# A planned order for all engines in a convolution and attention kernel

## The chip, the cores and the metric

The kernel runs on one core of a Trainium2 chip. The time is the device time of one execution in microseconds (us), as the median of several runs. The core has five engines that work side by side, each through its own list of instructions: TensorE (PE: matrix products; PEld: the loading of its weights), VectorE (DVE), ScalarE (ACT), GpSimd (POOL) and SyncE (SP), which here only issues DMA transfers.

## The reference

All numbers are 32-bit floats. The input x has 16 samples of 256 channels on a 32 by 32 picture, so 1024 tokens. Four layers follow each other; cut to what matters:

```python
def attention(x, ...):               # layers 0 and 2
    h = group_norm(x)                # 8 groups
    q, k, v = wq @ h, wk @ h, wv @ h
    a = softmax(q.T @ k / sqrt(256))
    return x + proj(a @ v)

def gate(x):                         # layer 1
    m, M = mean(x, channels), max(x, channels)
    r = relu(conv3x3([m, M], w1, b1))
    return x * sigmoid(conv3x3(m + M + r, w2, b2))

def clipped(x):                      # layer 3, q and k of 32 channels
    e = clip(q.T @ k / sqrt(32), -10, 10)
    return gamma * (v @ softmax(e).T) + x
```

## The kernel before, in words

The weights are folded first (`fold`): query and key weights of a layer become one matrix m, value and projection weights one matrix wvp, so that an attention needs the products x m (tiles t_l, in banks tb, ta, tc, tf), x wvp (vb, va, vc, vf), the logits (sb, sa, sc, sf) and the weighted sum (b, af, c). Each of these is a product of 2 by 2 blocks, done with seven block products instead of eight (`seven`, `weighted`); sums of blocks are made on VectorE ahead of it (`combine` at L924 to L927 for x, `logits` for t, `weighted` for the exponentials, `value_sums`). Nearly all products are recorded by one helper at L577. Their results lie in eight PSUM banks, and ScalarE (copies, L696 for logits, L765 to L781 for the weighted sum) and VectorE (additions, L627 and L749) bring them to SBUF.

Samples go through two streams, even and odd (`stream(0)`, `stream(1)`), the second 30 steps behind the first; `in_turn` records one step of each by turns. The program has constants (W_PLANES to W_AV3) that set how many steps a stage is held back. So the order in which the program records the products is tuned by hand. A repeat, in which each stream does one sample, takes about 329 us, and there are eight of them, less the ends.

Group normalisation (`group_norm`) is a chain of small instructions: bn_stats over x on VectorE (L114), aggregates (L117), transposes, rstd on GpSimd (L138), a_l and bb_l (L141 to L144) and the normalisation, half of x on VectorE (L147), half on ScalarE (L150). Between layers a sample goes to DRAM and back with another layout: `send` stores mid_x in four pieces and loads x (L536, L540). Each sample's x is loaded a second time in another layout, tokens xr (`load_tokens`, L470), to which the attention's results are added. The mean for the gate is made on ScalarE, row by row, into a scrap tile named junk (L1043).

At the start two weight matrices raw_l0 and raw_l2, w3 (printed as w), x of samples 0 and 1, small vectors vec, sc, vcol and qb, and an index tidx are loaded. `fold3` scales w3 (L414), copies parts of it into w3qk on GpSimd (L425) and makes biases; `build_toep` makes matrices for the 3 by 3 convolutions on GpSimd from tidx and sc (L85 to L103); `right_sums` makes sums of weight blocks on GpSimd or VectorE (L290 to L298). `in_strips` spreads a bias (strips, L395 and L403).

What sets the order: the framework's scheduler takes the recorded program and gives each engine a fixed list, in which it may move instructions past each other by its own estimates. Three pins limit it. `keep_in_program_order` holds single instructions (toeplitz rows, copies of weights, w3qk, the first statistics of sample 1) at their recorded place; `behind_folds` puts the normalisation of sample 0 on ScalarE behind the folded weights' copies; `in_traced_order` chains all instructions of the last sample's layer 3 on TensorE, VectorE and ScalarE in recorded order, which `ending()` writes out by hand: score products s (L1135), the copies t_qk (L1122 to L1128), its weighted sums b_end, af_end, c_end with acc_end (L1234), and the additions of biases to the stored tokens (L493).

Of the kernel before, what the change touches and what calls it, by code (L numbers as in the profile page):

```python
# [13 lines left out]
ALU = mybir.AluOpType  # L14
AX = mybir.AxisListType

P = 128
C = 256
CC = C // P
# [4 lines left out]
TPH = HALF // P  # L24
GROUP = 32
DQK = 32
G4 = P // DQK
PH = P // 2
# [11 lines left out]
L2_GAMMA, L2_BETA, L2_BQ, L2_BK, L2_BP = range(5, 10)  # L40
NVEC = 10
OFFSET = 30


W_PLANES, W_GATE1, W_GATE2, W_SEND1, W_NORM1, W_NORM2, W_NORM3, W_SEND2, W_EXP, W_AV, W_AV3 = 9, 1, 2, 4, 2, 10, 4, 7, 2, 2, 0
# [6 lines left out]
SIZES = 16384.0  # L52
REACH = 1.0
CHECKS = 3 + 2 * CC


class Const:
# [26 lines left out]
    def build_toep(self, tc, work, tidx):  # L84

        nc = tc.nc
        for k in range(3):
            for tap in range(9):
                w = self.sc[:, S_W1 + 9 * k + tap : S_W1 + 9 * k + tap + 1]
                if tap == 0:  # L90
                    one = self.toep[:, k, :]
                else:
                    one = work.tile([P, STRIP], FP, tag="tap", name=f"tap_{k}_{tap}")
                tc.keep_in_program_order(
                    nc.gpsimd.tensor_scalar(one, tidx, float(tap), w, ALU.is_equal, ALU.mult)
                )
                if tap:
                    nc.gpsimd.tensor_tensor(self.toep[:, k, :], self.toep[:, k, :], one, ALU.add)
            yield
        for g in range(1, NG):  # L100
            nc.gpsimd.tensor_copy(self.toep[:, 2 + g], self.toep[:, 2])
        nc.vector.tensor_scalar(self.neg_b2, self.sc[:, S_B2 : S_B2 + 1], -1.0, None, ALU.mult)
        yield  # L103


def group_norm(nc, k, small, xt, out, gamma, beta, nm, keep=None, parts=1, behind=None):

    st = small.tile([P, CC, 2, 6], FP, tag="st", name=f"st_{nm}", bufs=2)  # L110
    mv = k.moments
    for c in range(CC):
        for h in range(NH):
            first = nc.vector.bn_stats(st[:, c, h, :], xt[:, c, h * TPH : (h + 1) * TPH])  # L114
            if keep is not None:
                keep(first)
        nc.vector.bn_aggr(mv[:, 2 * c : 2 * c + 2], st[:, c, :, :])  # L117
    row = small.tile([P, GROUP], FP, tag="row", name=f"row_{nm}", bufs=2)
    nc.vector.transpose(row, mv)
# [20 lines left out]
    a = small.tile([P, CC], FP, tag="a", name=f"a_{nm}")  # L140
# [4 lines left out]
    for i in range(parts):  # L145
        ts = slice(i * NT // parts, (i + 1) * NT // parts)
        nc.vector.tensor_scalar(  # L147
            out[:, 0, ts], xt[:, 0, ts], a[:, 0:1], bb[:, 0:1], ALU.mult, ALU.add
        )
        other = nc.scalar.activation(  # L150
            out[:, 1, ts], xt[:, 1, ts], AF.Identity, bias=bb[:, 1:2], scale=a[:, 1:2]
        )
        if behind is not None:
            behind(other)
    yield


# [50 lines left out]
def fast_path(nc, tc, k, bad, x, w_l0, w_l2, w_l3, qk_bias, v_bias, tap_idx, out):  # L208
# [5 lines left out]

    B = x.shape[0]
    with ExitStack() as ctx:
        wts = ctx.enter_context(tc.tile_pool(name="wts", bufs=1))
        chan = ctx.enter_context(tc.tile_pool(name="chan", bufs=3))
        tokp = ctx.enter_context(tc.tile_pool(name="tokp", bufs=3))
        qkvp = ctx.enter_context(tc.tile_pool(name="qkvp", bufs=2))  # L220
        expp = ctx.enter_context(tc.tile_pool(name="expp", bufs=3))
        combp = ctx.enter_context(tc.tile_pool(name="combp", bufs=2))
        tcp = ctx.enter_context(tc.tile_pool(name="tcp", bufs=2))
        work = ctx.enter_context(tc.tile_pool(name="work", bufs=4))
        small = ctx.enter_context(tc.tile_pool(name="small", bufs=4))
        dram = ctx.enter_context(
            tc.tile_pool(name="dram", bufs=2, space=bass.MemoryType.DRAM)
        )
        ps_m = ctx.enter_context(
            tc.tile_pool(name="ps_m", bufs=8, space=bass.MemoryType.PSUM)  # L230
        )

        def bank(nm):
            return ps_m.tile([P, HALF], FP, tag="m", name=nm)
# [34 lines left out]
        w3 = wts.tile([P, CC, 2 * DQK + C], FP, name="w3")  # L269
# [3 lines left out]
        tidx = wts.tile([P, STRIP], FP, name="tidx")  # L273
# [26 lines left out]
        def whole(w, nm):  # L300

            full = work.tile([P, CC, C], FP, tag="oc", name=f"full_{nm}", bufs=3)
            tc.keep_in_program_order(nc.vector.tensor_copy(full, w))
            nc.vector.tensor_tensor(full[:, 0, P:], w[:, 1, P:], w[:, 0, P:], ALU.subtract)
            return full

        copied = []

        def fold(nm, which, base):


            w = raw[nm]
            wt = expp.tile([P, 3, CC, C], FP, tag="e", name=f"wt_{nm}")

            def transposed(j):
                for o in range(CC):
                    ps = bank(f"wtp_{nm}_{j}_{o}")
                    for c in range(CC):
                        nc.tensor.transpose(
                            ps[:, c * P : (c + 1) * P],  # L320
                            w[:, c, j * C + o * P : j * C + (o + 1) * P],
                            k.ident,
                        )
                    copy = nc.scalar.copy if nm == "l0" else nc.vector.tensor_copy
                    copied.append(copy(wt[:, j, o, :], ps[:, :C]))

            def multiplied(dst, left, right, scale):
                for c in range(CC):
# [82 lines left out]

        def fold3():

            tc.keep_in_program_order(  # L414
                nc.vector.tensor_scalar(
                    w3[:, :, :DQK], w3[:, :, :DQK], DQK**-0.5, None, ALU.mult
                )
            )
            for g in (0, G4 - 1):
                s = slice(g * DQK, (g + 1) * DQK)  # L420
                nc.vector.tensor_scalar(qb[s], qb[s], DQK**-0.5, None, ALU.mult)
            for i in range(2):
                for j in range(2):
                    tc.keep_in_program_order(
                        nc.gpsimd.tensor_copy(  # L425
                            w3qk[:, :, i, (i ^ j) * DQK : (1 + (i ^ j)) * DQK],
                            w3[:, :, j * DQK : (j + 1) * DQK],
                        )
                    )
            ps = bank("bias3")  # L430
            for c in range(CC):
# [7 lines left out]
            for o in range(CC):  # L439
                for c in range(CC):  # L440
# [4 lines left out]
                        start=(c == 0),  # L445
                        stop=(c == CC - 1),
                    )
            tc.keep_in_program_order(
                nc.vector.tensor_tensor(qb, ps[:, CC : CC + 1], qb, ALU.add)
            )  # L450
            nc.vector.tensor_tensor(bcol3, ps[:, :CC], vcol[:, 2, :], ALU.add)
            nc.vector.scalar_tensor_tensor(bcol3, bcol3, gam, bcol2, ALU.mult, ALU.add)
            in_strips(bcol3, bstrip3, "l3")
# [116 lines left out]
        def product(terms, fresh=True, lone=True):  # L570
# [4 lines left out]
            for i, (out, pairs) in enumerate(terms):  # L575
                for m, (left, right) in enumerate(pairs):
# [10 lines left out]
                    elif m == 0 and not lone:  # L587
# [5 lines left out]
                            ),  # L593
                            reason="the first product clears the bank's flags",
                        )

        def in_traced_order(start):

            engines = mybir.EngineType.PE, mybir.EngineType.DVE, mybir.EngineType.Activation
            before = {}  # L600
            for ins in nc.cur_bb.bb.instructions[start:]:
                if ins.engine not in engines:
                    continue
                if ins.engine in before:
                    tc.add_manual_dep(
                        ins,
                        before[ins.engine],
                        mybir.DependencyInfo(
                            mybir.DependencyClass.NoSync, mybir.DependencyReason.DATA
                        ),  # L610
                        reason="the last sample's order",
                    )
                before[ins.engine] = ins.name

        def seven(go, copy, block, banks, left, right):

# [196 lines left out]
        def alike(w, nm):  # L813


            sq = work.tile([P, HALF], FP, tag="oc", name=f"sq_{nm}", bufs=3)
            tc.keep_in_program_order(
                nc.vector.tensor_tensor(sq.rearrange("p (c o) -> p c o", c=CC), w, w, ALU.mult)
            )
            yield from pause()  # L820
            ps = bank(f"size_{nm}")
            for c in range(CC):
# [169 lines left out]
                then(h, tt.rearrange("p h c n -> p h (c n)"))  # L992
            count(ri, nm)

        def behind_folds(ins):

            tc.add_manual_dep(
                ins.ins,
                copied[-1].ins.name,
                mybir.DependencyInfo(  # L1000
                    mybir.DependencyClass.NoSync, mybir.DependencyReason.DATA
                ),
                reason="the weights' copies come first",
            )

        def head(b):

            fetch(b)
            xt = loaded.pop(b)
            by_chunk = xt.rearrange("p t c n -> p c t n")  # L1010
            xr = tokens[b] = load_tokens(b)
            keep = tc.keep_in_program_order if b == 1 else None
            yield from group_norm(
                nc,
                k,
                small,
                by_chunk,
                by_chunk,
                L0_GAMMA,
                L0_GAMMA + 1,  # L1020
                f"l0_{b}",
                keep,
                1 if b else NH,
                None if b else behind_folds,
            )
            ready[b] = xt, xr

# [68 lines left out]
        def clipped_attend(xt, y, lane, b):  # L1096
# [316 lines left out]
            if b == B - 1:  # L1413
                while running:
                    yield
                start = len(nc.cur_bb.bb.instructions)
                ending()
                in_traced_order(start)
                return

            steps = values(lane, left, right_of(*folded["l3"]), f"l3_{b}")
# [91 lines left out]
        for _ in in_turn([in_turn(streams), rest]):  # L1513
# [7 lines left out]
        nc.vector.tensor_scalar(  # L1521
            bad, some[0:1, :], -1.0, float(P * (3 * B * NT + CHECKS)), ALU.mult, ALU.add
        )


def general_path(nc, tc, k, x, w_l0, w_l2, w_l3, qk_bias, v_bias, out):
# [308 lines left out]
```

## Time and profile before

| | before |
|---|---|
| median of 3 runs | 2680.28 us (2677.83 to 2680.78) |
| the profiled execution's own time | 2683.05 us |
| its span | 2681.3 us |
| TensorE busy, weight loads busy | 99%, 88% |
| VectorE, ScalarE, GpSimd busy | 80%, 50%, 3% |
| granted TensorE clock | 0.997 of full speed |

A page of the profile gives the busy time of each engine, the chain of work that ended last, and groups of instructions by line and tile. A timeline lists instructions with start and duration, and in brackets how long the engine stood idle before and what released it. Tile names are cut at their numbers: x_0 and x_12 are both x, and t_l is the same tile for both attention layers. A matrix product in 32-bit floats has two records. Times of TensorE's ends are modelled, so distances between starts are the safer reading.

### The profile page before, as it was taken

Reading aid. Unit: us, or ns where it says so; the run is one execution under the profiler, and the core shown is the slowest. Engines: PE = TensorE matmul, PEld = TensorE weight load, DVE = VectorE, ACT = ScalarE, POOL = GpSimd, SP = SyncE. Lnnn points to the kernel's source line nnn. Section 1 sums busy time; section 2 is a strip of 40 time slices with the busy share of each in tenths; the row PEclk is TensorE's granted clock in tenths of the full one; section 3 lists DMA queues with packets and bytes.
Section 4 is the critical chain, followed back from the end, with each engine's and each line's share of the span. In section 5 each row is a group of like instructions: output and inputs, shape, how many; then the busy total and the mean of one; then the engine's idle time right before and its main releaser. Section 6 shows DMA issues by size and latency. Waiting matters only on the chain.

```text
span 2681.3 us, 47925 instructions
## 1 busy us (share of the span) xinstructions
PE 2646.6 (99%) x18998; PEld 2361.7 (88%) x18998; DVE 2149.9 (80%) x4180; ACT 1332.2 (50%) x2825; POOL 68.5 (3%) x172
## 2 busy tenths in 40 slices
PE   8999999999999999999999999999999999999998
PEld 7888898888988889989889898988989889898897
DVE  7888887888778887788867889678887788868776
ACT  4454455544465445554455544554454544545443
POOL 4100000000000000000000000000000000000000
PEclk9999999999999999999999999999999999999999
DMA  4021211212021120211201212112111121101111
GB/s 116 1 64 48 59 29 36 60 40 76 12 55 49 40 72 9 56 48 48 64 17 48 64 34 63 32 32 64 48 48 32 32 64 48 48 17 32 48 40 41
DMA packets 135878, 123.08 MB, mean 46 GB/s; under 512 B 12768, under 2 KB 126688, under 8 KB 135648
## 3 DMA queue, kind: packets, MB, share of 16 engines
q1 hardware_dynamic: 133776, 118.76, 16.1%
q8 instruction: 153, 2.51, 0.4%
q10 hardware_dynamic: 1872, 1.18, 0.1%
q14 instruction: 77, 0.63, 0.1%
HBM read 69.58 MB, written 50.33 MB: 45 GB/s over the span
## 4 chain that ended last, share of the span: by engine, by line
PE 89%; DVE 7%; ACT 1%; issue 1%; DMA 1%; POOL 0%; SPq 0%; DVEq 0%; ACTq 0%
PE b_l L577 16%; PE sb_l L577 12%; PE af_l L577 11%; PE c_l L577 11%; PE sc_l L577 8%; PE vb_l L577 5%; PE sf_l L577 4%; PE sa_l L577 4%; PE vc_l L577 3%; PE tb_l L577 3%; PE s L1135 2%; PE tc_l L577 2%; PE vf_l L577 2%; PE va_l L577 2%; PE qk L1109 1%
## 5 line engine op out<-in xcount | busy, mean ns | idle before, releaser
L577 PE MATMUL sb_l<-t_l,x 128*128 128x256 f32 x1024 | 255.9, 381 | 0.0
L577 PE MATMUL b_l<-vt,e_l 128*128 128x128 f32 x2048 | 250.1, 275 | 0.0
L577 PEld LDWEIGHTS b_l<-vt,e_l 128*128 128x128 f32 x2048 | 242.6, 192 | 4.9 <-DVE acc_l L749 2.3
L696 ACT COPY e_l<-sb_l 128x512 f32<-128x512 f32 x256 | 150.1, 586 | 141.9 <-PE sb_l L577 141.1
L706 ACT ACTIVATE e_l<-e_l 128x512 f32<-128x512 f32 x256 | 159.8, 631 | 121.7 <-DVE e_l L627 119.8
L577 PEld LDWEIGHTS sb_l<-t_l,x 128*128 128x128 f32 x1024 | 185.4, 191 | 32.2 <-issue 10.3
L708 ACT ACTIVATE e_l<-e_l 128x1024 f32<-128x1024 f32 x128 | 135.2, 1056 | 114.3 <-DVE e_l L627 113.6
L627 DVE TENSOR_TENSOR e_l<-sc_l,e_l 128x512 f32<-128x512 f32 x128 | 88.0, 687 | 125.4 <-PE sc_l L577 98.7
L577 PE MATMUL c_l<-tv,cb_l 128*128 128x129 f32 x1504 | 185.8, 276 | 0.0
L577 PEld LDWEIGHTS c_l<-tv,cb_l 128*128 128x128 f32 x1504 | 176.5, 191 | 6.8 <-issue 5.7
L627 DVE TENSOR_TENSOR e_l<-sb_l,e_l 128x512 f32<-128x512 f32 x256 | 165.7, 680 | 4.8 <-ACT e_l L696 0.5
L493 ACT ACTIVATE xr<-xr,bstrip 128x128 f32<-128x128 f32 (+1 forms) x376 | 138.1, 435 | 50.6 <-DVE xr L500 50.6
L773 ACT COPY acc_l<-af_l 128x256 f32<-128x256 f32 x94 | 34.8, 371 | 231.7 <-DVE acc_l L749 231.7
L1151 ACT ACTIVATE e<-s 128x512 f32<-128x512 f32 x256 | 131.5, 598 | 32.4 <-PE s L1135 31.7
L577 PE MATMUL sc_l<-t_l,xs_l 128*128 128x256 f32 x512 | 133.1, 382 | 0.3
L577 PE MATMUL sb_l<-tc_l,xs_l 128*128 128x256 f32 x512 | 132.9, 382 | 0.0
L577 PE MATMUL sf_l<-tc_l,x 128*128 128x256 f32 x512 | 132.5, 382 | 0.0
L577 PE MATMUL sc_l<-tc_l,xs_l 128*128 128x256 f32 x512 | 132.4, 381 | 0.0
L577 PE MATMUL af_l<-tv,e_l 128*128 128x128 f32 x1024 | 129.2, 277 | 2.3 <-ACT e_l L706 2.3
L577 PE MATMUL sa_l<-t_l,x 128*128 128x256 f32 x512 | 131.4, 379 | 0.0
L577 PE MATMUL b_l<-tv,e_l 128*128 128x128 f32 x1024 | 128.0, 275 | 0.0
L577 PEld LDWEIGHTS af_l<-tv,e_l 128*128 128x128 f32 x1024 | 120.5, 192 | 8.0 <-ACT e_l L706 4.9
(304 smaller groups left out, 5919.4 us busy)
## 6 DMA issues: line engine op xcount, KB each, us to landing
x<-mid_x SPq DMA_DIRECT2D x64, 512.0 KB, 3.3
xr<-in_x_dram SPq DMA_DIRECT2D x64, 256.0 KB, 5.2
mid_x<-t_z SPq DMA_DIRECT2D x128, 128.0 KB, 2.3
mid_x<-t_l SPq DMA_DIRECT2D x128, 128.0 KB, 2.3
x<-in_x_dram SPq DMA_DIRECT2D x62, 256.0 KB, 4.2
out_dram<-xr SPq DMA_DIRECT2D x124, 128.0 KB, 2.3
raw_l<-in_w_l_dram SPq DMA_DIRECT2D x1, 1024.0 KB, 7.9
raw_l<-in_w_l_dram SPq DMA_DIRECT2D x2, 256.0 KB, 6.0
```

Source lines behind the costliest of these rows:

```text
L493: nc.scalar.activation(y[:, s, ts], y[:, s, ts], AF.Identity, bias=bias[:, s : s + 1])
L577: mm = nc.tensor.matmul(out, left, right, start=fresh and m == 0 and (lone or i == 0), stop=(m == len(pairs) - 1), skip_group_check=True,)
L627: nc.vector.tensor_tensor(dst, src, dst, ALU.add)
L696: nc.scalar.copy(block(i, j), ps.rearrange("p (m n) -> p m n", m=2))
L706: nc.scalar.activation(part, part, AF.Exp)
L708: nc.scalar.activation(e[:, m : m + 2, :], e[:, m : m + 2, :], AF.Exp)
L773: nc.scalar.copy(acc[:, hi, c1], af[:, 1])
L1109: nc.tensor.matmul(ps[i * PH : (i + 1) * PH, : qt * P].rearrange("p (g n) -> p g n", g=qt), w3qk[:, c, i], xt[:, g0 : g0 + qt, c], start=( ...
L1135: nc.tensor.matmul(ss[g][:, j * 2 * P : (j + 1) * 2 * P].rearrange("p (t g j) -> p t g j", t=TPH, g=2), qk[gs, mh, 1 - blk, j * P : (j + 1 ...
L1151: nc.scalar.activation(by_strip[:, :, :, qa], ss[g].rearrange("p (m t n) -> p m t n", m=2, t=TPH), AF.Exp,)
```

## The change

All three pins are taken out. The pools of tiles are wrapped (`Book`, `Recorded`), so that it is known which tile takes which buffer. When the whole program is recorded, `Plan(nc, book).pin(tc)` runs:

- It reads every recorded instruction, finds by regions of tiles which ones depend on which, and gives each a time by a table (`durations`): how long its engine is taken and when its result is there. A DMA takes its queue for 60 ns and lands after 2.4 us (to DRAM), 3.4, 4.4 or, if it writes more than 1024 elements per partition, 7.0 us, whatever else is under way. GpSimd takes 500 ns and 2 ns for each element.
- It replays the program. TensorE takes its instructions strictly as recorded; of the other four engines, each takes what can start first, and of what can start within 1 ns of that, what has the lowest rank.
- Ranks come from the replay before: `needed` goes backwards through the dependencies and says when TensorE needs each result. There are three rounds, and the best by the plan's own time is kept.
- It chains the list of each engine, SP's DMA issues too, with edges that carry no semaphore: they fix the order in which the scheduler may place the instructions, and add no instruction and no wait.

No instruction is added, removed or changed in size. The core of the diff:

```diff
+        book = Book()
-        chan = ctx.enter_context(tc.tile_pool(name="chan", bufs=3))
+        chan = book.pool(ctx.enter_context(tc.tile_pool(name="chan", bufs=3)), 3)
...
-                tc.keep_in_program_order(
-                    nc.gpsimd.tensor_scalar(one, tidx, float(tap), w, ALU.is_equal, ALU.mult)
-                )
+                nc.gpsimd.tensor_scalar(one, tidx, float(tap), w, ALU.is_equal, ALU.mult)
...
-        if behind is not None:
-            behind(other)
...
-                start = len(nc.cur_bb.bb.instructions)
                 ending()
-                in_traced_order(start)
                 return
...
+        Plan(nc, book).pin(tc)
```

and of the new functions:

```python
def durations(engine, ins, outs, reads, mode):
    ap = outs[0].ap
    n, parts = elements(ap), ap[0][1]
...
    if ins.opcode == "DMACopy":
        if "DRAM" in str(outs[0].tensor.space):
            return 60, 2400
        if elements(outs[0].ap) > 1024:
            return 60, 7000
        return 60, 3400 if n == 1024 else 4400
    if engine == POOL:
        return 500 + 2 * n, 640 + 2 * n
...

    def run(self, rank):
...
        for _ in range(n):
            best = None
            if at < len(products) and not missing[products[at]]:
                r = ready(products[at])
                if r is not None:
                    best = max(free[PE], r), products[at]
            for e in (DVE, ACT, POOL, SP):
                times = [(max(free[e], r), i) for i in waiting[e] for r in [ready(i)] if r is not None]
                if times:
                    t = min(times)[0]
                    i = min((rank[i], i) for u, i in times if u <= t + 1)[1]
                    if best is None or t < best[0]:
                        best = t, i
...

    def needed(self, begin):
        need = [math.inf] * len(self.steps)
        for i in reversed(range(len(self.steps))):
            s = self.steps[i]
            if s.engine == PE:
                need[i] = begin[i]
                continue
            for j in s.ahead:
                other = self.steps[j].engine
                last = s.issue if other == s.engine else s.done + SEEN[other]
                need[i] = min(need[i], need[j] - last)
        return [(t, i) for i, t in enumerate(need)]

    def pin(self, tc):
        best, rank = None, [(0.0, i) for i in range(len(self.steps))]
        for _ in range(ROUNDS):
            found = self.run(rank)
            if best is None or found[0] < best[0]:
                best = found
            rank = self.needed(found[2])
        self.total = best[0]
        for order in best[1]:
            for i, j in zip(order, order[1:]):
                tc.add_manual_dep(
                    self.steps[j].ins,
                    self.steps[i].ins.name,
                    mybir.DependencyInfo(
                        mybir.DependencyClass.NoSync, mybir.DependencyReason.DATA
                    ),
                    reason="the planned order",
                )
```

## The prediction

> **What bounds the kernel now.** I read the page's head first, then the chain that ended last.
>
> ```profile
> span 2681.3 us, 47925 instructions
> PE 2646.6 (99%) x18998; PEld 2361.7 (88%) x18998; DVE 2149.9 (80%) x4180; ACT 1332.2 (50%) x2825; POOL 68.5 (3%) x172
> PE 89%; DVE 7%; ACT 1%; issue 1%; DMA 1%; POOL 0%; SPq 0%; DVEq 0%; ACTq 0%
> ```
>
> TensorE is busy throughout and 89% of the chain is its own. The diff leaves every instruction in place, so only TensorE's pauses can be won. I measured them from the start times of its matmul records: the usual start-to-start distance is 112 ns for 128 columns, 216 ns for 256, 429 ns for 512; what a step takes beyond that is a pause. Over the span these sum to 58.4 us: 16.3 in the first 175 us, 5.4 to 5.7 in each of seven repeats of 328.7 us (one sample in each stream), 6.1 after 2476 us. A perfect order gains less than 58 us. Of each repeat's 5.5 us, some 1.6 are restarts of about 0.1 us behind products that use part of the array, and stay. The rest has causes; TensorE's waits name them.
>
> ```profile
> PE tb_l L577 <- issue: 8.5, 8, 1.1
> PE tb_l L577 <- DVE xs_l L925: 3.0, 8, 0.4
> PE af_l L577 <- ACT e_l L706: 2.3, 8, 0.6
> ```
>
> Columns: total us, times, longest. Eight times each, so once a repeat and once more. The first is labelled "issue", but a timeline of TensorE and one of VectorE in the repeat at 1500 us show the real cause.
>
> ```profile
> 1522.72 1.12 PE L577 MATMUL sb_l<-tc_l,xs_l 128*128 128x256 f32 x4
> 1524.90 1.10 PE L577 MATMUL tb_l<-x,m_l 128*128 128x512 f32 x2 [1.06 <-issue]
> ```
>
> ```profile
> 1510.28 1.27 DVE L114 BATCH_NORM_STATS2 st_l<-x 128x6 f32<-128x512 f32 x2
> 1516.74 1.28 DVE L114 BATCH_NORM_STATS2 st_l<-x 128x6 f32<-128x512 f32 x2
> 1522.92 0.16 DVE L141 TENSOR_TENSOR a_l<-rstd_l,vec 128x2 f32<-128x2 f32 x1 [0.20 <-POOL rstd_l L138]
> 1523.99 0.81 DVE L147 TENSOR_SCALAR x<-x,a_l,bb_l 128x1024 f32<-128x1024 f32 x1
> ```
>
> The first product of the next attention reads x, and x is normalised until 1524.80; the product starts 0.10 us later. The norm chain stands between evictions on VectorE, so it takes 14 us. VectorE is not full (80%): this is order.
>
> The start is another matter. Here GpSimd, VectorE and TensorE are shown, then DMA issues of the first 60 us (KB each, us from issue to landing).
>
> ```profile
> 13.71 0.71 POOL L138 TENSOR_TENSOR rstd_l<-ve_l,neg_half 128x2 f32<-128x2 f32 x1 [11.46 <-DVE ve_l L134]
> 47.89 0.70 POOL L95 TENSOR_SCALAR toep<-tidx,sc 128x32 f32<-128x32 f32 x1
> ```
>
> ```profile
> 14.45 0.16 DVE L141 TENSOR_TENSOR a_l<-rstd_l,vec 128x2 f32<-128x2 f32 x1 [0.83 <-POOL rstd_l L138]
> 15.04 1.00 DVE L147 TENSOR_SCALAR x<-x,a_l,bb_l 128x512 f32<-128x512 f32 x2
> ```
>
> ```profile
> 17.05 1.10 PE L577 MATMUL tb_l<-x,m_l 128*128 128x512 f32 x2
> 46.29 0.55 PE L395 MATMUL strips_l<-bcol,ident 128*32 128x2 f32 x8 [0.93 <-DVE bcol L452]
> ```
>
> ```profile
> xr<-in_x_dram SPq DMA_DIRECT2D x12, 256.0 KB, 7.7
> tidx<-in_tap_idx_dram SPq DMA_DIRECT2D x3, 4.0 KB, 7.3
> raw_l<-in_w_l_dram SPq DMA_DIRECT2D x1, 1024.0 KB, 7.9
> ```
>
> GpSimd's rstd at 13.71 releases a_l, then the normalisation, then TensorE's first real work at 17.05. The toeplitz build comes much later, at 47.89. Nothing else covers TensorE at 14 to 17 us.
>
> **What the Trainium skill says.** "Perfetto Trace Analysis", Identifying the Most-Contended Engine: matmul occupancy overstates, weight-load occupancy is the better measure. Here 88% against 99%: the trace agrees that TensorE leads, and the pauses have to be taken from start times. Same page, Tensor Engine Instruction: ACT, DVE and GPSIMD execute strictly first in, first out. So an order pinned on GpSimd turns a wait of one instruction into a wait of all behind it; the trace agrees in that rstd starts 11.46 us after GpSimd's last work with nothing slipped in. "DMA: Bandwidth & Descriptors", Issuing engines are not separate DMA queues: all transfers interleave on the same 16 engines. Agrees: a 256 KB x load lands 4.2 us after issue in the median, the same size of xr in the crowded start 7.7 us. "TensorE: Matmul & The Clock Gate", What's actually happening: after an idle window of about 3.4 us TensorE runs at half clock. Agrees: 128-column records come 213 ns apart at 4.6 to 15.6 us.
>
> **The change, part by part.** The instruction sets are equal. Compared by order, 288 of 10,019 TensorE instructions move, 3084 of 4436 on VectorE (3.7 places in the mean), 1507 of 2757 on ScalarE, 84 of 188 on GpSimd, 71 of 655 on SP. The edges carry no semaphore, so they cost no instruction: 0 us for themselves; what they cost is the order they freeze.
>
> *Repeats, gain.* The norm chain moves 10 to 15 places up VectorE. Passing along its rows with their durations puts the end of L147 at 1515.4 instead of 1524.80, far before the 1523.6 at which TensorE would want it: 1.22 + 0.08 = 1.30 us gone. The combinations L924 to L927 come 2.5 to 4.4 us sooner, and the six pauses behind them in front of tb and tc at 1479 (0.54, 0.08, 0.09, 0.10, 0.28, 0.08) go: 1.16 us. ScalarE's copies of logits go ahead of the mean planes' rows (L1043), which removes 0.16 + 0.10 + 0.05 + 0.10 = 0.42 us before sc. The pauses before af (0.72 + 0.10 + 0.14 + 0.10 = 1.06 us) follow late exponentials (L706): their VectorE addition comes earlier, but the normalisation on ScalarE (1.23 us) now stands ahead of them; I take half, 0.53 us. Sum 3.4 us of 3.94.
>
> *Repeats, cost.* What the norm chain overtakes comes later. The worst is the eviction of bank b (L749), from 1515.91 to about 1522.0, needed by about 1525.4: 3.4 us of slack are left, so 0 by the pass. Such passes miss by a us or so, and several evictions move at once, so I set 0.6 us a repeat, estimated (bounds 0 and 3). Mid stores go ahead of an x load on SP: x is needed tens of us later, 0; without that cover, one load's 4.2 us, once a repeat. TensorE's own moves (two logits groups swap places) do the same work: 0. Net 2.8 us, seven times: 19.6. The stretches outside the repeats hold the same attention steps: 1.2 more after 50 us. Together -20.8 us (bounds -28 and -12, the repeat's gain between 3.8 and 1.5).
>
> *Start, cost.* The plan puts, on GpSimd, w3qk, then toep and two taps, then an addition, before rstd of sample 0. They read tidx, whose three loads now stand on SP behind raw_l2, w3, qb, sc, four loads of x_1 and four of xr. The plan prices every load alone (4.4 us; 7 for the largest), as if none shared. In the trace they do; its landing times give: what comes first is down at 11.0 us; raw_l2 takes 5.0 more; w3 0.84; qb and sc 0.8; x_1 4 x 0.78 = 3.1; xr 4 x 1.17 = 4.7; tidx 0.5. Sum 25.9 us. Then three tap rows of 0.7, one addition of 0.25 and rstd of 0.71: 29.0, where before it ended at 14.42. Some of this overlaps the landing, so 28 to 29. a_l moves from 14.45 to 28.5 or 29, TensorE's tb_l from 17.05 to 30 (+13). A cold restart is not new: TensorE ran at half clock there before. Behind it the work up to 46.29 is the same, with wt copies 2 us later relative to a_l but small waits (1.28, 0.93) less: I take +13.5 us (bounds +9 if transfers overlap better, +17.5 if lanes of the queue wait for each other). Nothing gives it back: the pauses of the next 80 us are only some 2 us.
>
> *Ending.* The hand order there is replaced too. The fourth bank's s no longer waits for copies of t_qk (2.12 us listed), but for an addition about 0.95 us before: -0.95. ScalarE's acc copy before b_end comes behind more additions: +0.5. Net -0.5 (bounds -2 and +1.5).
>
> *Sum.* +13.5 - 20.8 - 0.5 = -7.8 us against the profiled execution, 2683.05 (span 2681.3 and 1.75 around it): 2675.2. The median of the runs is 2680.28, 2.8 lower; the difference carries over: 2672.5, rounded 2672.
>
> **The rivals.** *A, slower: the evictions of VectorE become the wait in each repeat.* For: 3084 moves, the chain's first row waits for a reload from DRAM, and with the order frozen all evictions behind it wait too. Against: 3.4 us of slack. If the L749 eviction comes 3.0 us after its slack is used up, the cost bound of 3 is reached and the gain of a repeat is 0.4: 13.5 - 0.5 - 2.8 - 1.2 = +9.0, so 2689. It decides from where the gain of a repeat falls below (13.5 - 0.5 - 1.2)/7 = 1.7 us. *B: the start doesn't bite.* tidx is 12 KB in all; if it lands with its plan's time, rstd isn't held up: -21.3 gives 2659. Against: its place behind 5 MB of other loads. *C: the plan does not do what it says.* TensorE keeps its order nearly, and pauses might be its own; then only the start remains: +13, 2693. Against: tb's wait ends 0.10 us after x.
>
> **How the numbers follow.** Forecast 0.52 (2663 to 2681), A 0.23 (2682 to 2692), B 0.13 (2655 to 2663), C 0.12 (2691 to 2697). 0.2% is 5.4 us, about what this measurement can tell: faster below 2674.9, slower above 2685.6. Faster: 0.46 of the forecast and B's 0.13, 0.59. Slower: 0.15 of A and C's 0.12, 0.27. Same: 0.14. The range of 8 in 10 runs from B's middle to the lower part of C: 2660 to 2692; the forecast's own is 2663 to 2681.
>
> **What would show it.** At the start: rstd of sample 0 near 28 us and tb_l near 30; if tb_l is at 17 to 19, B. In repeats: tb_l's "issue" and xs_l waits gone, 8.5 and 3.0 us; a repeat of 325.9 us instead of 328.7; if new waits on acc or t_l evictions stand in the list with some 3 us each repeat, A. If the repeat stays at 328.7, C. I am wrong if the start loses under 9 us, or if a repeat gains under 1.5 or over 3.8.

## The result and the profile after

The changed kernel takes 2698.91 us (median of 6 runs, 2696.43 to 2703.0), the kernel before on the same chip 2680.65 us (6 runs, 2677.83 to 2682.13): 1.0070 times as long, 95% interval 1.0057 to 1.0083. I had forecast 2672. The profiled execution took 2701.25 us, 18.2 more than the one before. The head of its page, to be laid beside the three lines of before:

```profile
span 2699.4 us, 47923 instructions
PE 2644.2 (98%) x18998; PEld 2369.2 (88%) x18998; DVE 2195.8 (81%) x4180; ACT 1338.0 (50%) x2825; POOL 64.3 (2%) x172
PE 85%; DVE 6%; DMA 5%; ACT 2%; SPq 1%; issue 1%; POOL 0%; DVEq 0%; ACTq 0%; POOLq 0%
```

The work is the same. What is new is the chain: transfers had 1% of it and now have 5%. Where the 18.2 us lie is read from starts of products that both traces have. The first t_b product starts at 17.05 us before and at 29.36 after. The first product of sample 0's gate starts at 127.31 and 145.01: 17.7 us are lost by then. At the first q and k product of layer 3 (252.08 and 268.73) it is 16.65, so 1.05 has been won. From this product to the same one seven repeats later it is 328.68 us a repeat before and 328.95 after: 1.9 lost in seven repeats. The rest, to the end of the execution, is 0.3 shorter. 17.7 - 1.05 + 1.9 - 0.3 = 18.2 to within rounding. So the start costs more than I said, and the repeats, which were to win 2.8 us each, win nothing: of the 26.0 us between forecast and measurement they make 21.5, the start 4.2. The granted clock is not the reason in the repeats: it is 1.00 in both traces from the first of these products to the last.

TensorE's waits after (total us, times, longest), against the three lines of before:

```profile
PE tb_l L862 <- DVE x L439: 15.5, 1, 15.5
PE af_l L862 <- ACT e_l L973: 11.9, 8, 1.5
...
PE fold_l L622 <- DVE wt_l L616: 4.4, 1, 4.4
PE sb_l L862 <- ACT e_l L963: 3.8, 7, 0.7
PE s L1386 <- ACT e L1402: 2.1, 4, 0.8
PE sc_l L862 <- ACT e_l L963: 1.8, 4, 1.0
```

The two old rows on tb_l (8.5 and 3.0 us) are gone, as forecast. But af_l, which was to fall from 2.3 to about half, has grown to 11.9, and sb_l, sc_l and, in layer 3, s for exponentials are new. The gain was made and spent again within the same repeat. (Line numbers are those of the changed kernel: L577 is now L862, L627 L894, L696 L963, L706 L973, L114 L408, L147 and L150 L439 and L442, L138 L430.)

**The start**, first GpSimd, then TensorE:

```profile
14.43 0.52 POOL L713 COPY w3qk<-w 128x64 f32<-128x64 f32 x2 [12.60 <-DMA w<-in_w_l_dram]
26.04 0.41 POOL L390 TENSOR_SCALAR toep<-tidx,sc 128x32 f32<-128x32 f32 x1 [11.09 <-DMA tidx<-in_tap_idx_dram]
...
27.36 0.72 POOL L430 TENSOR_TENSOR rstd_l<-ve_l,neg_half 128x2 f32<-128x2 f32 x1
```

```profile
29.36 2.07 PE L862 MATMUL tb_l<-x,m_l 128*128 128x512 f32 x2 [15.49 <-DVE x L439]
```

GpSimd stands 11.09 us in front of a row of the toeplitz build, because the 12 KB of tidx, issued at 17.7 to 19.2 us behind all that the prediction lists, land at 25.2 to 25.8; and rstd, whose input was ready at 12.3, stands behind it.

**A repeat**, first VectorE, then ScalarE, then TensorE, then SP's issues around 1470 us:

```profile
1473.99 0.69 DVE L894 TENSOR_TENSOR e_l<-sc_l,e_l 128x512 f32<-128x512 f32 x1 [0.33 <-PE sc_l L862]
1475.50 0.69 DVE L408 BATCH_NORM_STATS2 st_l<-x 128x6 f32<-128x512 f32 x1 [0.82 <-DMA x<-mid_x]
1476.12 1.27 DVE L894 TENSOR_TENSOR e_l<-sb_l,e_l 128x512 f32<-128x512 f32 x2
1478.28 0.69 DVE L408 BATCH_NORM_STATS2 st_l<-x 128x6 f32<-128x512 f32 x1 [0.89 <-DMA x<-mid_x]
1478.89 0.67 DVE L894 TENSOR_TENSOR e_l<-sa_l,e_l 128x512 f32<-128x512 f32 x1
```

```profile
1480.13 0.57 ACT L963 COPY e_l<-sb_l 128x512 f32<-128x512 f32 x1
...
1483.79 1.24 ACT L442 ACTIVATE x<-x,bb_l,a_l 128x1024 f32<-128x1024 f32 x1
1484.93 1.13 ACT L973 ACTIVATE e_l<-e_l 128x512 f32<-128x512 f32 x2
```

```profile
1480.75 1.13 PE L862 MATMUL sb_l<-t_l,x 128*128 128x256 f32 x4 [0.62 <-ACT e_l L963]
...
1485.60 1.60 PE L862 MATMUL af_l<-tv,e_l 128*128 128x128 f32 x12 [1.49 <-ACT e_l L973]
```

```profile
1467.84 3.92 SPq L821 DMA_DIRECT2D mid_x<-t_z  x8
1471.92 2.52 SPq L825 DMA_DIRECT2D x<-mid_x  x2
```

Two statistics of the reloaded x stand between additions of logits, and VectorE waits 0.82 and 0.89 us for their transfers. Whatever stands behind them is up to 1.7 us later: additions, the exponentials and copies on ScalarE that follow them, and the products. In the whole profile it is 21 such waits; before, no statistic waited for a reload:

```profile
DVE st_l L408 <- DMA x<-mid_x: 17.5, 21, 1.9
```

SP's rows say why the plan put them there. An issue takes SP 0.30 to 0.45 us, where the plan has 0.06: the eight stores take 3.92 us, not 0.5. The two reloads land 3.56 and 4.15 us after issue, where the plan has 3.4. On ScalarE there is a second suspect: the other half of the normalisation (L442, 1.24 us) stands in front of two exponentials that af waits for.

### The profile page after: what moved, and what is told of

Read it like the earlier page. It is cut to its first block, busy times and chain, and to the rows that moved or that the text cites. A ratio compares the mean times of both kernels' runs of the same rounds, so it can differ in the third digit from the quotient of the medians.

```text
span 2699.4 us, 47923 instructions
## 1 busy us (share of the span) xinstructions
PE 2644.2 (98%) x18998; PEld 2369.2 (88%) x18998; DVE 2195.8 (81%) x4180; ACT 1338.0 (50%) x2825; POOL 64.3 (2%) x172
## 4 chain that ended last, share of the span: by engine, by line
PE 85%; DVE 6%; DMA 5%; ACT 2%; SPq 1%; issue 1%; POOL 0%; DVEq 0%; ACTq 0%; POOLq 0%
PE b_l L862 17%; PE af_l L862 12%; PE c_l L862 11%; PE sb_l L862 11%; PE sc_l L862 7%; PE vb_l L862 4%; PE sf_l L862 4%; PE sa_l L862 4%; PE tb_l L862 3%; PE vc_l L862 2%; PE s L1386 2%; PE tc_l L862 2%; DMA x<-mid_x 1%; PE va_l L862 1%; PE vf_l L862 1%
## 5 line engine op out<-in xcount | busy, mean ns | idle before, releaser
L862 PE MATMUL sb_l<-t_l,x 128*128 128x256 f32 x1024 | 257.2, 383 | 3.8 <-ACT e_l L963 3.8
L862 PE MATMUL b_l<-vt,e_l 128*128 128x128 f32 x2048 | 250.1, 275 | 0.0
L862 PEld LDWEIGHTS b_l<-vt,e_l 128*128 128x128 f32 x2048 | 242.6, 192 | 4.9 <-issue 2.3
L973 ACT ACTIVATE e_l<-e_l 128x512 f32<-128x512 f32 x256 | 158.3, 628 | 136.2 <-DVE e_l L894 135.0
L862 PEld LDWEIGHTS sb_l<-t_l,x 128*128 128x128 f32 x1024 | 185.5, 191 | 39.0 <-issue 10.3
L963 ACT COPY e_l<-sb_l 128x512 f32<-128x512 f32 x256 | 149.7, 585 | 126.2 <-PE sb_l L862 124.8
L862 PE MATMUL c_l<-tv,cb_l 128*128 128x129 f32 x1504 | 185.8, 276 | 0.0
L894 DVE TENSOR_TENSOR e_l<-sc_l,e_l 128x512 f32<-128x512 f32 x128 | 87.9, 687 | 117.0 <-PE sc_l L862 88.8
L862 PEld LDWEIGHTS c_l<-tv,cb_l 128*128 128x128 f32 x1504 | 176.5, 191 | 6.8 <-PE qk L1360 3.1
L894 DVE TENSOR_TENSOR e_l<-sb_l,e_l 128x512 f32<-128x512 f32 x256 | 164.1, 680 | 4.0 <-PE sb_l L862 2.0
L862 PE MATMUL af_l<-tv,e_l 128*128 128x128 f32 x1024 | 127.7, 276 | 11.9 <-ACT e_l L973 11.9
L862 PE MATMUL sc_l<-t_l,xs_l 128*128 128x256 f32 x512 | 133.1, 383 | 2.0 <-ACT e_l L963 1.8
L862 PEld LDWEIGHTS af_l<-tv,e_l 128*128 128x128 f32 x1024 | 120.0, 192 | 16.5 <-ACT e_l L973 13.4
L862 PE MATMUL sc_l<-tc_l,xs_l 128*128 128x256 f32 x512 | 132.4, 381 | 0.0
L862 PE MATMUL sf_l<-tc_l,x 128*128 128x256 f32 x512 | 131.9, 380 | 0.0
L862 PE MATMUL sb_l<-tc_l,xs_l 128*128 128x256 f32 x512 | 131.5, 379 | 0.0
L862 PE MATMUL sa_l<-t_l,x 128*128 128x256 f32 x512 | 131.4, 379 | 0.0
L1045 ACT COPY acc_l<-c_l 128x258 f32<-128x258 f32 x94 | 35.0, 373 | 194.3 <-PE c_l L862 194.3
L862 PE MATMUL c_l<-vt,e_l 128*128 128x129 f32 x1024 | 125.6, 275 | 0.0
```

Of the source, the lines that this page charges most:

```text
L862: mm = nc.tensor.matmul(out, left, right, start=fresh and m == 0 and (lone or i == 0), stop=(m == len(pairs) - 1), skip_group_check=True,)
L894: nc.vector.tensor_tensor(dst, src, dst, ALU.add)
L963: nc.scalar.copy(block(i, j), ps.rearrange("p (m n) -> p m n", m=2))
L973: nc.scalar.activation(part, part, AF.Exp)
L1045: nc.scalar.copy(acc[:, hi, P:], c)
```

## The experiments

All are the changed kernel with small edits, and the runs of each are compared with runs of the kernel before on the same chip. "A repeat" is measured as above, in the profile of each kernel; that of before is 328.68 us, that of the changed kernel 328.95.

**True prices for stores and reloads.**

```diff
-            return 60, 2400
+            return 430, 2400
-        return 60, 3400 if n == 1024 else 4400
+        return (340, 4200) if n == 1024 else (60, 4400)
```

> The changed kernel with two prices of the plan set to what its trace shows: a store to DRAM takes SP 430 ns (plan: 60), and the reload of x takes SP 340 ns and lands after 4.2 us (plan: 60 ns and 3.4 us). Theory: the plan thinks x back too early, so VectorE is pinned to wait for it (17.5 us in 21 waits of the statistics) while additions of logits that are ready stand behind; with true prices these waits go, sb's and af's pauses (0.9 and 1.75 us a repeat) shrink to under 0.8 together, and the time falls from 2699 to about 2682 (2679 to 2687), start unchanged with tb_l at 29.4 us. Rival (the pauses come from ScalarE's normalisation of x ahead of the exponentials, not from the wait): statistics wait less, but the repeat stays within 0.7 us of 328.9, time 2694 or more.

2672.49 us, ratio to before 0.9964 (0.9952 to 0.9976); 26.4 us less than the changed kernel, where about 17 were expected; a repeat is 325.77 us, 3.2 less. The order of TensorE, GpSimd and SP is that of the changed kernel; on VectorE each first statistic goes behind two additions, and on ScalarE the normalisation goes behind the exponentials. Other instructions move with them: 66 in all on VectorE, 28 on ScalarE. VectorE's and TensorE's waits:

```profile
DVE st_l L408 <- DMA x<-mid_x: 6.5, 12, 0.9
```

```profile
PE af_l L862 <- ACT e_l L973: 1.6, 4, 0.7
```

The two numbers are enough to give the repeats the gain forecast. But both suspects went away together, so which one it was is not told yet. Nor were the prices tried apart; by size the issues weigh more (3.92 us instead of 0.5 for eight stores, against landings 0.2 and 0.75 us later than priced).

**The reload without waiting for its stores, order kept.** The load reads from the input instead of mid_x; a dependency known only to the plan keeps its order.

```diff
-                mid.rearrange("h p g n -> p h (g n)"),
+                x[0].rearrange("(h p) n -> p h n", h=NH)[:, halves],
```

> The changed kernel with the order of every engine kept instruction for instruction, but the reload of x reads from the input instead of from the stores just made, so it needn't wait for them (the layers after the first get other data: the gate's result is left out of what follows). Theory: VectorE's waits for the reload nearly go with no order changed; sb's pause goes and af's falls to 0.3 to 0.9 us a repeat; 1.5 to 2.2 us a repeat, so about 2685 (2682 to 2689). Rival (ScalarE's normalisation of x ahead of the exponentials is what holds af): sb's pause goes, af's stays above 1.3 us; 2692 or more.

2698.72 us (ratio 1.0068, 1.0052 to 1.0085): nothing won. The time is within the rival's "2692 or more", but af's wait, 10.0 us in 8, has come down to 1.25 each, just below the 1.3 that the rival needs. The edit didn't do what it was made for:

```profile
1476.15 0.69 DVE L415 BATCH_NORM_STATS2 st_l<-x 128x6 f32<-128x512 f32 x1 [2.23 <-DMA x<-in_x_dram]
...
1477.94 0.68 DVE L415 BATCH_NORM_STATS2 st_l<-x 128x6 f32<-128x512 f32 x1
```

Both reloads now went out together, at 1470.93 and 1471.37, and landed 5.2 and 6.0 us later, both under way at once. The second wait went and the first grew from 0.82 to 2.23 us. It speaks for the wait, since the pause went with it (it moved from sb to sc: 9.6 us in 8), but it settles nothing.

**No wait for the reload, order kept.** The four statistics take the tokens xr, which are in SBUF; the plan still orders them as if they read x.

```diff
-            nc.vector.bn_stats(st[:, c, h, :], xt[:, c, h * TPH : (h + 1) * TPH])
+            src = xt[:, c, h * TPH : (h + 1) * TPH] if of is None else of[:, c * NG : (c + 1) * NG, h * TPH : (h + 1) * TPH]
+            nc.vector.bn_stats(st[:, c, h, :], src)
```

> The changed kernel with the order of every engine kept instruction for instruction, but the statistics before layer 2 are taken from the tokens xr, which are in SBUF, instead of from the reloaded x, so these four instructions wait for no transfer (the normalisation uses other statistics than it should; all else is computed from it). Theory (VectorE's wait for the reload delays the logits' additions behind it): the waits st from mid_x go (17.5 us in 21 before), sb's pause goes and af's falls from 1.65 to 0.3 to 0.9 us a repeat; 1.5 to 2.4 us a repeat, so about 2684 (2680 to 2688). Rival (ScalarE's normalisation ahead of the exponentials holds af): af's pause stays above 1.3 us, 2692 or more.

2680.12 us (0.9996, 0.9987 to 1.0004), a repeat 326.86 us: 2.1 less than in the changed kernel, and the traces have every engine's instructions in the same order. The statistics' waits on mid_x are gone from the list, and so is sb's. So the wait for the reload is shown to cost 2.1 us a repeat. A remainder of af stays, 0.7 us each time:

```profile
PE af_l L870 <- ACT e_l L981: 5.8, 8, 1.0
```

**ScalarE's normalisation behind the exponentials, the wait left in.** In the finished order, for each x of layer 2:

```diff
+                act[at : at + 3] = act[at + 1 : at + 3] + [i]
...
+                dve[at : at + 3] = dve[at + 1 : at + 3] + [s1]
```

The second line moves VectorE's first sum of x, which reads what ScalarE has normalised, behind two sums of exponentials.

> The changed kernel with one swap in its order, twice a repeat: on ScalarE the normalisation of x goes behind the two exponentials that stand after it, and on VectorE the first sum of x goes behind the two sums of exponentials; waits for the reload stay. Theory (the wait is the cause): af's pause falls by at most 0.7 us, from 1.65, sb's stays; 0.3 to 0.7 us a repeat, so 2694 to 2698. Rival (ScalarE's normalisation is the cause): af's pause falls under 0.5 us, 2690 or less.

2715.81 us (1.0133, 1.0116 to 1.0150), which neither theory allows. The swap also fell on a second place of a repeat where VectorE's sum of x could not go back with it:

```profile
DVE xs_l L1210 <- ACT x L463: 24.4, 8, 3.4
```

A new wait of 3 us a repeat hides what was asked. With the swap only where VectorE's sum follows:

> The swap of the run before, but only at the one place of a repeat where VectorE's sum of x can go back with it (in the run before the swap at the other place made VectorE wait 3 us a repeat for ScalarE, so it told nothing of the time). Theory (two causes in series: the wait for the reload, 2.0 us a repeat by the run with other statistics, and ScalarE's normalisation ahead of the exponentials, the rest): af's pause falls from 1.65 to 0.9 to 1.2, 0.5 to 1.0 us a repeat, 2691 to 2696. Rival (the normalisation is no cause at all): nothing is won, 2698 or more.

2690.89 us (1.0036, 1.0022 to 1.0050), a repeat 328.04: 0.9 less. af falls from 11.9 to 7.7 us in 8:

```profile
PE af_l L877 <- ACT e_l L988: 7.7, 8, 1.0
```

So the second suspect, together with VectorE's sum that hangs on it, is a cause too, the smaller one; the two moves were not tried apart.

**Both removed.** The statistics from xr and that one swap:

> The statistics from xr (no wait for the reload; the normalisation uses other statistics than it should) and that one swap together, all else in the order of the changed kernel. Theory: both causes removed, af's pause nearly gone, the repeat at 325.8 us as with the true prices; 2673 (2669 to 2677). Rival (a third cause, as VectorE's order between the additions): 2678 or more.

2677.79 us (0.9988, 0.9982 to 0.9995), 0.8 above the expected range and 0.2 below where the rival's begins; its profiled execution took 2675.57. I go by the repeat in that profile, since the start differs (the gate's first product at 142.2 to 145.1 us in eight profiles with this start): 326.10 us, 2.85 less. 2.1 and 0.9 make 3.0, so the two add up. 0.3 us a repeat lie between this and the true prices, so there is a third cause, a small one. TensorE's waits show where:

```profile
PE s L1409 <- ACT e L1425: 2.1, 3, 1.2
...
PE af_l L885 <- ACT e_l L996: 0.2, 1, 0.2
```

With the true prices the list has no wait of s for e: 2.1 us in seven repeats are the 0.3. What delays e was not tried.

**The index priced late.** One price, for the 32-column load of tidx:

```diff
-        return 60, 3400 if n == 1024 else 4400
+        return 60, {1024: 3400, 32: 20000}.get(n, 4400)
```

> The changed kernel with one price of the plan changed: the index tidx lands after 20 us instead of 4.4. Theory: the toeplitz build in front of rstd on GpSimd is the whole start loss; rstd of sample 0 starts at 15 us, the first product tb_l at 16 to 17.5 us instead of 29.4, and the time falls by 11 to 16 us to about 2685. Rival (the crowded start costs elsewhere, as in the 4.4 us wait for copies wt_l): tb_l comes early but the wait grows, and less than 7 us is won, 2692 or more. Repeats unchanged at 328.9 us.

2686.57 us (1.0018, 1.0012 to 1.0025): 12.3 less. GpSimd and TensorE:

```profile
14.68 0.76 POOL L430 TENSOR_TENSOR rstd_l<-ve_l,neg_half 128x2 f32<-128x2 f32 x1
```

```profile
16.74 2.07 PE L862 MATMUL tb_l<-x,m_l 128*128 128x512 f32 x2 [2.88 <-DVE x L439]
```

The first product is back at 16.74 us. The gate's first product is at 131.88 us, 13.1 better than in the changed kernel and still 4.6 behind before. Of the rest, 1.9 is the wait of fold_l for copies wt_l, 3.2 us here and 1.3 before. The trace places the rest: TensorE runs at half clock from 16.7 to 21.9 us and from 39.1 to 42.4. Up to the transposes wtp_l at 23.27 us (21.11 before) that costs 2.5 us, in the eight records of fold_l 1.5; the start of tb_l and later steps win 1.3 back.

**Both prices.**

> Both price changes at once. Theory: the two losses are independent, gains add: 2699 less 17 less 14, about 2667 (2662 to 2674), faster than the kernel before by 0.3 to 0.7%. Rival (a plan of all engines gains nothing in the repeats beyond what it loses, whatever its prices): repeats stay at 328.7 us or more and the time at 2680 or more.

2659.92 us (0.9923, 0.9907 to 0.9940): 39.0 less than the changed kernel and below the expected range. The two edits alone won 26.4 and 12.3. They add up, and the losses are independent.

**A price too high.** As the first experiment, the reload at 8.0 us.

```diff
+        return (340, 8000) if n == 1024 else (60, 4400)
```

> As the kernel with stores at 430 ns, but the reload of x priced at 8.0 us instead of 4.2, far above what it takes. Theory: a price too low is dear (everything behind waits), a price too high is nearly free while x has slack: 2670 to 2676, no waits of the statistics. Rival: there is no such slack, the chain of the norm comes too late and tb's pause of before returns (1.3 us a repeat), 2680 or more.

2686.70 us (1.0026, 1.0015 to 1.0036), a repeat 326.99. I was wrong that lateness is nearly free: no statistic waits for the reload, but smaller waits come in tb_l for t_l (2.0 us in 8) and in the gate's c_l for rows (3.6 us in 8), and the last sample's vc_end waits 3.7 us. So the rival's time came (2680 or more), but not by tb's pause of before, for x. A price 3.8 us too high costs 1.2 us a repeat; the plan's own, too low, cost 3.2.

**One wire for all transfers.** In place of the prices, an issue takes 430 ns and bytes go one after another:

```diff
+        return 430, 2000 + 4 * elements(outs[0].ap) * ap[0][1] / 245
...
+            if s.ins.opcode == "DMACopy":
+                end[i] = max(end[i], wire[0] + s.done)
+                wire[0] = end[i] - 2000
```

> The changed kernel with one model in place of all prices of transfers: an issue takes 430 ns, a transfer takes its bytes at 245 bytes per ns on one wire that all share, and lands 2.0 us after that. Theory: both losses have one cause, transfers priced as if alone; the one model mends the start (tb_l at 16 to 18 us) and the repeats (326 us), as the two single prices did; about 2659 (2655 to 2664). Rival (the prices mended only what they were fitted to): one of the two losses stays, 2670 or more.

2657.40 us (0.9913, 0.9896 to 0.9930), the fastest of all; a repeat is 325.56. TensorE's waits on the two culprits of the start:

```profile
PE tb_l L861 <- DVE x L438: 3.5, 1, 3.5
PE fold_l L621 <- DVE wt_l L615: 2.0, 1, 2.0
```

The first product starts at 16.87 us, and the gate's first product at 130.74, 3.4 behind before instead of 17.7. One model mends most of the start and all of the repeats: the cause in both is transfers priced as if alone and as if an issue cost SP next to nothing. The last 3.4 us of the start were not removed; the trace has TensorE at half clock from 18.0 to 21.4 and from 38.5 to 41.8 us, and fold_l's wait is 0.7 longer than before.

**The same with one round**, so that ties go by traced order and not by TensorE's need:

```diff
-ROUNDS = 3
+ROUNDS = 1
```

> The kernel with the one shared wire, but with one round of planning, so that what can start is taken in traced order and not by when TensorE needs it. Theory (what is won in the repeats comes from the ranks): pauses come back, 2670 or more. Rival (taking what is ready first is enough, ranks decide little): 2656 to 2662.

2717.16 us (1.0136, 1.0119 to 1.0153), a repeat 332.44, worse than before by 3.8. Additions of the combined exponentials now come late for b:

```profile
PE b_l L861 <- DVE e_l L1034: 22.6, 16, 3.0
```

So the ranks carry what is won in the repeats: 6.9 us a repeat lie between the two.

## Why the prediction failed, point by point

- **Who bounds and what can be won: right.** TensorE's pauses were all there was to win. With the transfers priced right, the plan wins 2.9 to 3.1 us a repeat (325.8 and 325.6 against 328.68); I had put 2.8.
- **Repeats, gain: right for tb.** The waits of tb_l for x and xs_l left the list. **Wrong for af:** "I take half" of 1.06 us. It rose to 1.75 a repeat (1.65 + 0.10). **Not there for sc:** instead of 0.42 us less, sc_l has new waits.
- **Repeats, cost: here the prediction failed.** I set 0.6 us "(bounds 0 and 3)" for evictions that the norm chain overtakes, and took the eviction of bank b, L749, with its 3.4 us of slack, as the worst. The net gain measured was -0.27 us, so against a gain of 3.41, taken as forecast, the cost was 3.7. It did not sit there: b's waits for acc are 0.4 us in the whole profile. It sat in the additions of logits next to the chain's first rows, and came from a transfer. The step that failed is the term that I put at nothing: "Mid stores go ahead of an x load on SP: x is needed tens of us later, 0". After the first 60 us SP's two orders differ in nothing but this: two of the eight stores go ahead of the first reload, once for each sample. That x is what the chain starts from, and even before it was needed 9 us after its load was issued, not tens:

```profile
1450.17 3.82 SPq L536 DMA_DIRECT2D mid_x<-t_z  x6
1454.22 0.34 SPq L540 DMA_DIRECT2D x<-mid_x  x1
...
1459.01 0.34 SPq L540 DMA_DIRECT2D x<-mid_x  x1
```

```profile
1463.31 1.28 DVE L114 BATCH_NORM_STATS2 st_l<-x 128x6 f32<-128x512 f32 x2
```

The two halves land at 1458.25 and 1462.38, 8.1 and 12.2 us behind the first store's issue, and the first statistics stand at 13.1. After, they land at 7.6 and 10.4, no later; but the first statistic stands at 7.7, its wait of 0.82 included. So the stores did not delay x; what is wrong is the reason, that x is needed much later. The chain was moved up by 5.5 us, into the landing. My figure for the case without that cover, 4.2 us a repeat, was the nearer one. I had named the mechanism in rival A ("the chain's first row waits for a reload from DRAM, and with the order frozen all evictions behind it wait too"), but priced it at the wrong eviction; and I had used the argument that the plan prices every load alone for the start, and not for the repeats.
- **Repeats, split.** 2.1 us for VectorE's wait (order kept, wait removed), 0.9 for ScalarE's normalisation ahead of two exponentials (order swapped, wait kept), 2.85 for both together, 3.2 with true prices. The last 0.3 us are waits of layer 3's s; their cause stays open.
- **Start: mechanism right, size nearly.** Foretold: rstd done at 28 to 29 us, tb_l at 30, +13.5 us (bounds +9 and +17.5). Measured: 28.08, 29.36, and +17.7 by the gate's first product in the profile (+14.9 to +17.8 in eight kernels with this start). The run with tidx priced late gives 13.1 of it to the toeplitz build. tb_l came 12.3 us late, as foretold (+13); what I mis-sized lies behind it. I had the copies wt_l "2 us later relative to a_l but small waits (1.28, 0.93) less". They came 3.3 us later relative to it, and the wait for them grew from 1.28 to 4.39: +3.1. And I put cold restarts at nothing, as "not new". Before, TensorE was at full clock again by 15.6 us (the spacing of 213 ns that I read at 4.6 to 15.6 us stands there only at 4.6 to 6.1 and 12.3 to 13.0). Now its first pairs take 2.07 and 1.63 us instead of 1.10 and 1.02: +1.5 by starts. Behind the wait for wt_l it happens again, which before it did not:

```profile
35.31 1.99 PE L331 MATMUL fold_l<-raw_l,wt_l 128*128 128x256 f32 x8 [1.28 <-DVE wt_l L325]
37.15 1.03 PE L577 MATMUL sb_l<-t_l,x 128*128 128x256 f32 x4
```

```profile
52.27 3.18 PE L622 MATMUL fold_l<-raw_l,wt_l 128*128 128x256 f32 x8 [4.39 <-DVE wt_l L616]
55.24 1.57 PE L862 MATMUL sb_l<-t_l,x 128*128 128x256 f32 x4
```

That is another 1.7. 12.3 + 1.5 + 3.1 + 1.7 = 18.6; 0.9 is won back before the gate, most of it from smaller waits for w3qk and bcol.
- **Ending: right.** -0.3 us from the last such product on, -0.5 foretold. As foretold, s waits less for t_qk (0.9 us instead of 2.1) and b_end more for acc_end (0.7 instead of 0.5).
- **Rivals.** C's sum (2693, only the start remains) came nearest, and its sign too (the repeat stays at 328.7), for a wrong reason: TensorE's pauses were not its own. A's reason was the nearest, though its sign, waits on acc or t_l, did not come; with the cost of a repeat at 3.7 instead of 3.0 and the start at 17.7 instead of 13.5 its sum is 2680.28 + 17.7 - 0.5 - 1.2 + 1.9 = 2698.
- **A slip without weight.** The parts of TensorE's pauses (16.3, seven times 5.4 to 5.7, 6.1) make 60 to 62 us, not 58.4.

## What to carry to other kernels

An order frozen by a plan is as good as the plan's prices for what it can't see: an instruction that is put too early on an engine that works in order holds all that is ready behind it, so before a chain is moved up, look up when its first input lands, and don't take the time at which it was needed in the old order. Here a few wrong lines on transfers turned a gain of 0.9% into a loss of 0.7%, and a wrong price in the other direction cost about a third as much a repeat. When two losses show up, ask first whether one wrong assumption makes both: one shared wire mended most of the start and the repeats at once.

## What the runs showed of the hardware

- A DMA issue on SP held it for 0.30 to 0.45 us in the repeat shown, so eight stores in a row took 3.9 us of SP, and a reload that stands behind them went out only then.
- Two loads of 512 KB issued 0.44 us apart (from the input) landed 5.2 and 6.0 us after issue; issued 2.2 us apart (from mid_x), 3.56 and 4.15. Letting a transfer start earlier moved the wait here instead of removing it.
- A stop of TensorE costs beyond its length. After 15.5 us of idleness the first two pairs of 512-column records took 2.07 and 1.63 us instead of 1.10 and 1.02; after 4.4 us, eight records of 256 columns took 3.18 instead of 1.99. The granted clock in the trace is 0.50 from 20.0 to 32.4 us and from 52.9 to 56.3. "TensorE: Matmul & The Clock Gate" of the Trainium skill, What's actually happening, has the reason (an idle clock passes half its pulses), and the trace agrees.
